# Two stages per slot for the layer tails while the third layer's table is being completed, and one everywhere else

## The chip, the core and the metric

The kernel runs on one core of a Trainium2 chip. The metric is the device time of one execution in microseconds. Inside the core five engines run side by side[...]: TensorE (PE, matrix products), VectorE (DVE), ScalarE (ACT), GpSimd (POOL, which here issues the indirect DMAs and a few small powers) and SyncE (SP, which issues plain DMAs). They wait for each other through semaphores.

## What is computed

Four graph layers follow each other over 8 batches of 2048 nodes with 128 features. The adjacency matrix is sparse: each of its 2048 x 2048 entries is one with probability 1/128, so a node has about 16 neighbours. Layers 0 and 1 are attention layers with 8 heads, a feed-forward part and two layer norms; layers 2 and 3 are graph attention layers with one layer norm.

```python
# layers 0 and 1
scores = jnp.einsum('bnhd,bmhd->bhnm', Q, K) / jnp.sqrt(HEAD_DIM)
scores = jnp.where(mask, -jnp.inf, scores)
attn_out = jnp.einsum('bhnm,bmhd->bnhd', softmax(scores), V)
x = layer_norm(h + (attn_out @ Wo + bo), ln1_g, ln1_b)
x = layer_norm(x + relu(x @ W1 + b1) @ W2 + b2, ln2_g, ln2_b)
# layers 2 and 3
h = x @ W
e = leaky_relu((h @ a_src)[:, :, None] + (h @ a_dst)[:, None, :])
att = softmax(where(adj == 0, -inf, e))
x = ln_gamma * norm(att @ h + x) + ln_beta
```

## The kernel before

The kernel never forms the dense score matrix. At the start it finds the neighbours of every node and sorts the nodes by their number of neighbours. A **tile** t (0 to 15) is 128 nodes of that order, all 8 batches with them; `CAPS` says how many neighbour slots a tile has, 30 for tile 0 down to 11 for tile 15. Each layer l has a **table** in device memory with one row per node (`tables[l]`): keys and values for layers 0 and 1 (2048 numbers), projected features and scores for layers 2 and 3 (1040 numbers). A tile gathers the rows of its neighbours, slot by slot, with an indirect DMA on POOL (`gather`, L320), and works on them.

**Chunks.** The list `every` holds all the work of the four layers in order, cut into chunks: up to 2 neighbour slots in layers 0 and 1, up to 4 in layers 2 and 3. A chunk lies in one of six buffers kv0 to kv5, used in turn. A chunk of layers 2 and 3 (`gat_chunk`) has the stages: small weights and one large product on DVE (L745 to L757), eight scalings by ACT (L762, two batches of each slot), one sum on DVE (L766), and eight matrix products with the identity on PE that add into PSUM (L772).

**Tails.** When a tile's chunks are done, DVE scales the sum (L643 in layers 0 and 1, L649 in layers 2 and 3) and a tail turns it into rows of the next layer's table. A tail is a Python generator, and each `yield` ends one stage. In layers 0 and 1 (`attention_tail`) two halves of a tile (four batches each) run as two tails, the second three stages behind: transposes on PE (L329), a copy on ACT (L666), the residual sum on PE (L674, L678), squares on ACT (L471), a power on POOL (L476, written `rs`), scaling on ACT (L480), transposes, copy (L686), feed-forward (L691, L696, L702 to L712), the second norm (again L471, L476, L480), transposes, copy (L720), projection (L521 to L536) and copies into `rows` (L541 to L547, ACT). In layer 2 (`gat_tail`) one tail does both halves: sums on PE (L793 to L802), squares (L809), one power for both (L836), scaling (L817), transposes, copies (L824) and the same projection. `state_done` then stores the state and loads a later tile's through SP, and `put_rows` writes the rows into the table with an indirect DMA on POOL (L494, called a scatter below) and counts it in `put[l + 1]`. `rows` has one buffer.

**Order.** The order of all instructions is written out by hand. `layers` goes through the chunks; for each it runs stages of the chunk and its neighbours and calls `slot` three times. `slot` (L1103) advances every thread and every tail by one stage and calls `fetch`, which issues the gathers of chunks some four ahead. In the kernel before, every third slot advances the tails once more if `hurry` (L1098) says so: in the last tile of layer 2, and in layers 2 and 3 as long as the table that the layer reads is not complete.

**The start of a layer.** `fetch` does not issue a gather before enough of the table is written. Because most of the table is there when a layer begins, `ORDER` and `EARLY` put first those slots of tiles 0 and 1 whose neighbours lie in the tiles already written. The first eight chunks of layers 2 and 3 are called C1 to C8 here:

- C1, C2, C3, C4: eight slots each of tile 0 and tile 1; they need 13 tiles in the table.
- C5: four slots of tile 0; it needs tile 13 too (14 tiles).
- C6, C7: four slots of tile 0 and of tile 1; they need tile 14 too (15 tiles).
- C8: the folded slots of tile 0 (two gathers); it needs tile 15, so the whole table, as does all that follows.

A scatter into a table waits until all gathers from that table issued before it have landed, and a gather waits until the last scatter before it has landed; `order` below always means the order in an engine's queue. C1 lies in kv2 in layer 2 and in kv5 in layer 3, and the next chunks take the next buffers.

Of the kernel before, what the change touches and what calls it, by code (L numbers as in the profile page):

```python
# [19 lines left out]
NT = N // P  # L20
# [62 lines left out]
def sparse_path(ctx: ExitStack, tc: tile.TileContext, ins: dict, out: bass.AP, flag: bass.AP):  # L83
# [978 lines left out]
    put = [NT, 0, 0, 0]  # L1062
    every = []
    blocks = [[{} for _ in range(NT)] for _ in range(4)]
    for l in range(4):
        per = 2 if l < 2 else 4
        for t, k, ns, folded in pieces(l, per):
            c = dict(l=l, t=t, k=k, ns=ns, folded=folded, box=blocks[l][t])
# [1 line left out]
            c["run"] = (attention_chunk if l < 2 else gat_chunk)(l, c)  # L1070
            every.append(c)
    now = [0, 0]
    beat = [0]

    def advance(group):
        for g in list(group):
            if next(g, 0) == 0:
                group.remove(g)

    def fetch():  # L1080

        while now[1] < len(every):
            c = every[now[1]]
            l, t, k, ns = c["l"], c["t"], c["k"], c["ns"]

            if now[1] - now[0] > (4 if now[1] >= KVB and every[now[1] - KVB]["l"] > 1 else 3):
                return
            resorted = l > 0 and t < 2 and not c["folded"]
            need = NT - max([b for end, b in EARLY[t] if k + ns <= end] + [0] if resorted else [0])
            if put[l] < need:  # L1090
                return
            c["buf"] = buffer()[:, : ns * width(l)].rearrange("p (s c) -> p s c", s=ns)
            for i in range(ns):
                at = t * BASE if resorted else first[t]
                index = (sorted_lists if resorted else lists)[:, at + k + i : at + k + i + 1]
                gather(l, index, c["buf"][:, i])
            now[1] += 1

    def hurry():

        c = every[min(now[0], len(every) - 1)]
        return c["l"] == 2 and c["t"] == NT - 1 or c["l"] > 1 and put[c["l"]] < NT

    def slot():
        advance(threads)
        advance(tails)
        fetch()
        beat[0] += 1
        if beat[0] % 3 == 0 and hurry():
            advance(tails)  # L1110

    def drain():
# [40 lines left out]
    def layers():  # L1153
# [7 lines left out]
        for i in range(len(every) + 2):  # L1161
# [3 lines left out]
            if c["k"] == 0:  # L1165
                l, t = c["l"], c["t"]
                if l == 0:
                    if t + 2 < NT:
                        threads.append(find_lists(t + 2))
                    if t == 0:  # L1170
                        state(0, 1)
                        threads.append(later(12, lambda: state(0, 2) or iter(())))
                        threads.append(later(12, clear_late))
                    if t in (2, 6):
                        threads.append(order_lists(t // 4))
                while l < 2 and "asked" not in c["box"]:
                    slot()
            while i < len(every) and now[1] <= i:
                slot()
# [11 lines left out]
            if c1["l"] in (2, 3) and c1["last"]:  # L1191
                sums(c1["l"], c1["t"], c1["box"])
            go(c)
            slot()
            go(c)
            slot()
# [533 lines left out]
```

## Time and profile before

| | us |
|---|---|
| three runs | 3429.68, 3435.46, 3435.26 (median 3435.26) |
| profiled execution | 3404.58 |
| its span, first to last instruction | 3402.8 |
| mean granted TensorE clock | 0.918 |

Busy time of the engines in three stretches of the profiled execution:

| stretch | from, to (us) | DVE | PE | ACT | POOL | DMA share |
|---|---|---|---|---|---|---|
| inside layer 1 | 1900 to 2000 | 99.32 | 91.78 | 40.09 | 65.41 | 0.79 |
| first product of C1 to first product of C8, layer 2 | 2230.79 to 2327.27 | 44.44 | 65.80 | 45.24 | 40.14 | 0.53 |
| about the same in layer 3 (2788.99 to 2870.17) | 2789 to 2870 | 41.91 | 57.17 | 34.75 | 37.61 | 0.60 |

The numbers under an engine's name are its busy microseconds in the stretch; the share of DMA is the mean of the core's 16 DMA engines. An indirect DMA on POOL is shown with the time in which POOL issues it; its data land later.

### The profile page before, as it was taken

To read this page: it belongs to the slowest core of one execution; us is meant where nothing else is said; L and a number is where in the kernel's file an instruction comes from. 1 tells how busy PE (TensorE), PEld (TensorE's weight loads), DVE (VectorE), ACT (ScalarE), POOL (GpSimd) and SP (SyncE) were. 2 spreads that over 40 slices of the span, in tenths; PEclk is the share of its full clock that TensorE was granted. 3 is DMA by queue.
4 is the path that set the end of the run, shared out by engine and by line. 5 is a ranking of instruction groups with operands and counts; after the bars stand their busy time and mean duration, and the time that the engine had idled before them with its cause. 6 is when DMAs were issued, how large, how long until landed. Compare 5 with 4: busy or idle time off the path is not lost.

```text
span 3402.8 us, 34669 instructions
## 1 busy us (share of the span) xinstructions
PE 2743.1 (81%) x10618; PEld 1582.9 (47%) x10618; DVE 3058.3 (90%) x2695; ACT 1426.6 (42%) x4972; POOL 2207.9 (65%) x1453
## 2 busy tenths in 40 slices
PE   5647888878989997788888989986888976667675
PEld 4523445545555553455545555653445543233332
DVE  7789999999999999999999999976788866889885
ACT  5711333334444442233333444543555654444444
POOL 0065788588657655455676666646787865788773
PEclk9878999999999998899999999998899988888887
DMA  8587787888888777688887888767999986899883
GB/s 336 188 333 266 292 292 282 314 298 288 308 315 299 290 262 295 226 328 295 303 321 295 295 309 299 265 206 250 321 352 346 347 327 223 292 314 330 300 284 112
DMA packets 200625, 986.52 MB, mean 290 GB/s; under 512 B 31918, under 2 KB 33712, under 8 KB 128436
## 3 DMA queue, kind: packets, MB, share of 16 engines
q0 software_dynamic: 175024, 890.45, 72.4%
q1 hardware_dynamic: 20502, 75.52, 5.9%
q10 hardware_dynamic: 4904, 18.24, 1.4%
q8 instruction: 87, 1.43, 0.2%
q14 instruction: 108, 0.88, 0.1%
HBM read 937.16 MB, written 91.55 MB: 302 GB/s over the span
## 4 chain that ended last, share of the span: by engine, by line
DVE 32%; PE 25%; issue 18%; DMA 10%; POOL 5%; ACT 3%; POOLq 0%; DVEq 0%; ACTq 0%
DVE kv L620 11%; DVE kv L606 11%; PE acc L630 8%; PE acc L772 6%; DMA kv<-table,lists 4%; POOL kv L320 3%; DMA kv<-table,sorted_lists 3%; DVE sc L609 2%; PE m L712 2%; DVE kv L766 2%; DMA table<-rows,perm 2%; DVE kv L757 2%; PE m L329 2%; DVE sums L455 1%; DMA out_dram<-rows,perm 1%
## 5 line engine op out<-in xcount | busy, mean ns | idle before, releaser
L320 POOL DMA_INDIRECT kv<-table,lists x955 | 1450.0, 1518 | 357.2 <-issue 206.7
L630 PE MATMUL acc<-kv,ident 128*128 128x512 f32 x2200 | 1107.7, 634 | 222.1 <-DVE kv L620 221.9
L772 PE MATMUL acc<-kv,ident 128*128 128x512 f32 x1184 | 610.1, 667 | 188.6 <-DVE kv L766 155.4
L630 PEld LDWEIGHTS acc<-kv,ident 128*128 128x128 f32 x2200 | 413.7, 202 | 655.1 <-issue 367.5
L606 DVE TENSOR_TENSOR kv<-kv,q 128x2048 f32<-128x2048 f32 (+1 forms) x282 | 629.2, 2231 | 18.7 <-DMA kv<-table,lists 9.7
L609 DVE TENSOR_REDUCE sc<-kv 128x128 f32<-128x2048 f32 (+1 forms) x284 | 634.0, 2232 | 9.2
L620 DVE TENSOR_TENSOR kv<-kv,w 128x2048 f32<-128x2048 f32 (+1 forms) x284 | 631.4, 2223 | 4.9 <-ACT w L615 4.8
L772 PEld LDWEIGHTS acc<-kv,ident 128*128 128x128 f32 x1184 | 243.6, 215 | 504.7 <-issue 285.1
L757 DVE TENSOR_TENSOR kv<-kv,pair 128x3072 f32<-128x3072 f32 (+1 forms) x150 | 466.1, 3108 | 1.0
L476 POOL TENSOR_TENSOR rs<-ss,half 128x4 f32<-128x4 f32 x128 | 221.2, 1728 | 325.4 <-ACT n L471 324.6
L766 DVE TENSOR_TENSOR kv<-kv 128x2048 f32<-128x2048 f32 (+1 forms) x150 | 296.0, 1974 | 129.0 <-ACT kv L762 129.0
L762 ACT ACTIVATE kv<-kv,ws 128x128 f32<-128x128 f32 x1108 | 339.0, 406 | 163.7 <-DVE ws L751 105.5
L471 ACT ACTIVATE n<-m,eps 128x128 f32<-128x128 f32 x512 | 181.0, 366 | 427.1 <-PE m L712 217.4
L615 ACT ACTIVATE w<-sc,lmask 128x64 f32<-128x64 f32 x554 | 165.0, 351 | 455.3 <-DVE sc L609 454.7
L320 POOL DMA_INDIRECT kv<-table,sorted_lists x153 | 204.9, 1339 | 113.0 <-PE acc L630 41.3
L480 ACT ACTIVATE n<-m,rs 128x128 f32<-128x128 f32 x512 | 146.0, 370 | 109.4 <-POOL rs L476 109.0
L494 POOL DMA_INDIRECT table<-rows,perm x57 | 100.2, 1758 | 134.6 <-ACT rows L545 33.5
L329 PE MATMUL m<-ident,n 128*128 128x128 f32 x640 | 106.2, 288 | 73.5 <-ACT n L817 57.2
L712 PE MATMUL m<-w_L_w,hT 128*128 128x128 f32 x1024 | 156.2, 275 | 0.0
L329 PEld LDWEIGHTS m<-ident,n 128*128 128x128 f32 x640 | 82.3, 147 | 140.6 <-ACT n L817 69.0
L712 PEld LDWEIGHTS m<-w_L_w,hT 128*128 128x128 f32 x1024 | 134.9, 192 | 0.0
L691 PE MATMUL m<-n1T,w_L_gnn_W 128*128 128x512 f32 x256 | 131.5, 597 | 0.8 <-ACT n1T L686 0.4
(241 smaller groups left out, 3459.5 us busy)
## 6 DMA issues: line engine op xcount, KB each, us to landing
kept<-xT SPq DMA_DIRECT2D x48, 512.0 KB, 7.4
xT<-kept SPq DMA_DIRECT2D x48, 512.0 KB, 6.8
kv<-in_adj_dram SPq DMA_DIRECT2D x16, 1024.0 KB, 6.7
table<-kv ACTq DMA_DIRECT2D x16, 1024.0 KB, 5.0
kv<-table,lists POOLq DMA_INDIRECT x955, 7.1
kv<-in_x_nodes_dram SPq DMA_DIRECT2D x16, 512.0 KB, 5.8
kv<-table,sorted_lists POOLq DMA_INDIRECT x153, 6.3
found<-cand POOLq DMA_DIRECT2D x16, 64.0 KB, 4.0
```

Source lines behind the costliest of these rows:

```text
L320: nc.gpsimd.indirect_dma_start(out=dst, out_offset=None, in_=tables[l][:, :], in_offset=bass.IndirectOffsetOnAxis(ap=index, axis=0), bound ...
L329: nc.tensor.transpose(pt[:, j * P : (j + 1) * P], src[:, j, :], ident)
L476: nc.gpsimd.tensor_tensor(rs, ss, half[:, :4], op=ALU.pow)
L606: nc.vector.tensor_mul(kk, kk, q[:, None].to_broadcast([P, ns, NB, D]))
L609: nc.vector.tensor_reduce(sc[:, :ns].rearrange("p s (b h) -> p (s b) h", h=NH), kk.rearrange("p s b (h j) -> p (s b) h j", h=NH), axis=AX. ...
L620: nc.vector.tensor_mul(vv, vv, w[:, k : k + ns, :].rearrange("p s (b h) -> p (s b) h", h=NH)[:, :, None, :] .to_broadcast([P, ns * NB, HD, ...
L630: nc.tensor.matmul(acc[:, j, :], merge if c["folded"] else ident, kv[:, i, 4 * j : 4 * j + 4, D:], start=k + i == 0, stop=c["last"] and i ...
L712: nc.tensor.matmul(y[:, j, :], hT[:, f, j, :], wt["2"][:, f, :], start=False, stop=f == 1, skip_group_check=True,)
L757: nc.vector.tensor_mul(hv[:, :, :nv, :], hv[:, :, :nv, :], wc[:, :, :nv, None].to_broadcast([P, ns, nv, D]))
L762: nc.scalar.mul(hv[:, i, b, :], hv[:, i, b, :], ws[:, i, b - nv : b - nv + 1])
L766: nc.vector.tensor_add(hv[:, : ns - left], hv[:, : ns - left], hv[:, left:ns])
L772: nc.tensor.matmul(acc[:, j, :], merge if c["folded"] else ident, hv[:, i, 4 * j : 4 * j + 4, :], start=k + i == 0, stop=c["last"] and i = ...
```

## The change

`hurry` and the counter `beat` go. The tails now take a second stage in every slot, and not in every third, while the current chunk is one of layer 2 and layer 2's table is not complete. In the last tile of layer 2 and at the start of layer 3 they take one stage per slot. Counted over the whole program, the second stage is taken 15 times before (7 at the start of layer 2, 3 in its last tile, 5 at the start of layer 3) and 17 times after, all at the start of layer 2. No operation is added or left out: the change only reorders instructions within the queues of PE, ACT, POOL and SP. DVE's order is the same.

```diff
     now = [0, 0]
-    beat = [0]
...
-    def hurry():
-
-        c = every[min(now[0], len(every) - 1)]
-        return c["l"] == 2 and c["t"] == NT - 1 or c["l"] > 1 and put[c["l"]] < NT
-
     def slot():
         advance(threads)
         advance(tails)
         fetch()
-        beat[0] += 1
-        if beat[0] % 3 == 0 and hurry():
+
+        if now[0] < len(every) and every[now[0]]["l"] == 2 and put[2] < NT:
             advance(tails)
```

## The prediction

> **What bounds the kernel now.** I read the page's busy slices first, then the busy time by stretch, then the waits and the chain of waits at the two places where DVE drops.
>
> ```profile
> DVE  7789999999999999999999999976788866889885
> ...
> DMA  8587787888888777688887888767999986899883
> ```
>
> DVE is at 90% or more nearly everywhere in layers 0 and 1. It falls in slices 27 to 29 (2210 to 2470 us) and 33 to 34 (2720 to 2890 us), where layers 2 and 3 begin; DMA falls with it, so neither is the limit there. By stretch (PE, PEld, DVE, ACT, POOL):
>
> ```profile
> 2230.79:2327.27 96.48, 65.80 (x318) 42.41 (x316) 44.44 (x41) 45.24 (x171) 40.14 (x39) 0.86 0.53 176
> 2789.00:2870.00 81.00, 57.17 (x222) 32.43 (x220) 41.91 (x37) 34.75 (x140) 37.61 (x29) 0.87 0.60 211
> ```
>
> No engine is full: both stretches are chains of latency, 52 and 39 us of DVE idle. The waits in the first, then the second stretch:
>
> ```profile
> DVE kv L745 <- DMA kv<-table,lists: 23.7, 1, 23.7
> POOL rs L476 <- ACT n L471: 23.4, 3, 12.0
> ...
> POOL table L494 <- DMA kv<-table,sorted_lists: 7.9, 1, 7.9
> ```
> ```profile
> DVE kv L766 <- ACT kv L762: 40.7, 7, 10.8
> PEld m L329 <- ACT n L817: 30.7, 3, 12.5
> ACT n L817 <- POOL rs L836: 30.7, 3, 13.0
> ...
> POOL table L494 <- ACT score L547: 13.6, 1, 13.6
> ```
>
> In layer 2 DVE waits 23.7 us for C8's gathers, so for the scatter of tile 15. In layer 3 almost all comes from one thing: ACT stands at L817 until POOL has done the power L836, and everything behind it on ACT waits, L762 first. POOL is late because gathers stand ahead of the power and wait for a scatter. POOL's timeline shows it (the last column is its idle time and what ended it):
>
> ```profile
> 2803.94 1.01 POOL L494 DMA_INDIRECT table<-rows,perm  x1 [7.36 <-DMA kv<-table,sorted_lists]
> 2804.97 1.67 POOL L836 TENSOR_TENSOR rs<-ss,half 128x8 f32<-128x8 f32 x1
> ...
> 2820.58 2.33 POOL L494 DMA_INDIRECT table<-rows,perm  x1 [5.96 <-ACT rows L545]
> 2828.54 1.03 POOL L320 DMA_INDIRECT kv<-table,sorted_lists  x1 [5.63 <-DMA table<-rows,perm]
> ...
> 2839.88 1.67 POOL L836 TENSOR_TENSOR rs<-ss,half 128x8 f32<-128x8 f32 x1
> 2855.12 2.36 POOL L494 DMA_INDIRECT table<-rows,perm  x1 [13.56 <-ACT score L547]
> ```
>
> The scatters are those of tiles 13, 14, 15, the powers those of tiles 14 and 15. Tile 15's squares end at 2830.3 (ACT's timeline), its power runs 9.6 us later, behind C6's and C7's eight gathers; from there to its scatter are 15.2 us.
>
> **What the Trainium skill says.** "Perfetto Trace Analysis", section "DMA Instruction — SWDGE (GPSIMD)": the profiler's end of such a DMA is when the last descriptor is generated, not when the data have moved. The trace agrees: scatters of 1.0 to 2.4 us on POOL release their readers 4.3 (at 2267.88) to 7.2 us (at 2820.58) after the start. "TensorE: Matmul & The Clock Gate", section "Architectural detail: the array is 16× 32×32, not 1× 128×128", under "Engine queue depths": ACT, DVE and each GpSimd core are strict FIFO. So a power behind gathers waits for them: L836 starts at 2839.88, 0.02 us after the last of the eight.
>
> **The change part by part.** Only queues are reordered; the built program shows the orders. POOL at the start of layer 3 (g is four gathers, s a scatter, p a power; numbers are tiles):
>
> ```
> before: s12 gC1 p13 gC2 gC3 gC4 s13 p14 gC5 s14 gC6 gC7 p15 s15 gC8
> after:  s12 gC1 p13 gC2 gC3 gC4 p14 s13 gC5 p15 s14 gC6 gC7 s15 gC8
> ```
> and at the start of layer 2 (two halves: a, b; the second norm has a prime):
> ```
> before: p14'b gC5 s14 p15a gC6 gC7 p15b p15'a p15'b s15 gC8
> after:  p14'b gC5 s14 gC6 gC7 p15a p15b p15'a p15'b s15 gC8
> ```
>
> *Start of layer 3* (times on the old axis; the two orders are the same up to 2779.92, the first L817 of tile 13). Each tail stage falls behind a later chunk, and the powers 14 and 15 move ahead of a scatter.
> - ACT after its first L817 (1.14 us) does L762 of tile 15's second chunk (2.44) at once: done 2783.4, so DVE's L766 starts 2.2 us earlier than 2785.60. PE then loses its later gaps of 6.1 and 11.6 us (at 2807.10 and 2842.01, both for L817).
> - s13 stays at 2803.9: it waits for C4's gathers, the last issued at 2795.58 and landing 7.56 us later. p14 needs squares at 2796.7 and runs in that wait, free.
> - s13's landing (2808.1) frees the one `rows` buffer. Then on ACT: L541 to L547 0.9, L824 0.6, L762 2.4, L809 1.4, L541 0.5; PE L793 to L802 1.9; ACT L809 1.5; POOL p15 1.7: 2808.3 + 10.9 = 2819.2, so s14 goes at about 2819.5 against 2820.58, 1.1 earlier. C5's gathers have landed (2813.63 + 5.54 = 2819.2). o of tile 15 (L649), at 2814.28 before behind the L329 that waited for L817, now needs only PE's sums of the last chunk, about 2803, so it does not hold p15.
> - From s14 the last of the eight gathers is issued 18.3 us later as before (2820.58 to 2838.87), now 2837.8. The 13.56 us of waiting for tile 15's rows go; what is late next is the landing of C7's gathers, 8.1 us as the chain shows for four gathers (2258.97 to 2267.08): 2845.9. The rows are ready before: L762 of C6 stands ahead of the last L541 on ACT and waits for C6's gathers (last issued 2832.6, landed 2840.7), then 0.9 + 2.4 + 0.9 = 2844.9. Margin 1.0.
> - s15 2845.9 against 2855.12: 9.2 us. C8 follows 14.85 us after s15 (2855.12 to DVE at 2869.97), and DVE has C7 done by 2853. I take **-9.2**. Bounds: the landing of s14 has been 4.3 to 9.3 us (2763.18) where I use the 7.2 of the old s14: -2.9, +2.1; p15 late by 3 us through PE running its matmuls at the slow rate after a pause (L772 x8 took 6.10 at 2808.14 against 3.60): +3. So -12 to -4.
>
> *Last tile of layer 2*: the three stages given up move only copies and squares around L762; POOL's order there is the same and s12 waits for a DMA. Nothing, with the wait of p13 behind s12 as cover; without it 2 us (one slot, a third of a 6.2 us chunk: 0.55 small products, 3.35, 2.29).
>
> *Start of layer 2*: the table is complete five slots earlier in the code; what counts is the queues.
> - p14'b: with both L696 ahead of C1's L762 (2.44), ACT is at L480 and L471 at 2252.0 instead of 2252.6. gC5 and s14 are 0.6 earlier: s14 2267.3.
> - Tile 15's first power now stands behind the eight gathers: 2283.9, not 2268.92. The second, at 2284.43 before, comes after ACT's first L480 and second L471 (1.1 + 1.4): about 2287.5. ACT stands still meanwhile, C4's L762 behind it, until 2289.7 (2271.0 before).
> - From the first power: scaling 1.1, squares 1.4, L686 0.6, power 1.05, scaling 1.1, L762 2.4, two L696 and L686 1.9: 2293.7. Then PE: C3's L772 to 2294.8, L702 to L712 3.0, two L691 1.8, L696 0.6, L702 to L712 3.0: 2303.2; ACT C5's L762 and L471 to 2305.5; power 1.05, scaling 1.15: 2307.8; PE's projection is through L527 at 2308.2; ACT L541 to L547 1.4, L720 0.6, C6's L762 2.4, L541 to L545 0.9: rows at about 2313.6. s15 2313.9 against 2314.22.
> - So the stages gained are given back by the powers' place on POOL: **-0.3**. Bounds: each ACT-PE handover may hold 0.3 us more, some ten of them, and PE may run slow for one L772 more: +5; PE at full rate from the start: -4. The delayed L762 push C3 to C7 on DVE, done by 2315, and DVE waits for C8 to 2326: that cover is 11 us.
>
> *SP*: each moved stage 20 takes a state's store and load with it, 0.32 us of issue each, tiles ahead of use; nothing. The rest of layers 2 and 3 keeps its order and shifts as a whole.
>
> Sum: -9.2 - 0.3 = -9.5 on the profiled execution of 3404.58: 3395.1. That execution is 0.9% below the median of the runs, so in the same ratio 3435.26 x 3395.1 / 3404.58 = **3425.7**.
>
> **Rivals.**
> - *Both starts gain.* Layer 2's table really comes five slots earlier: 5 x 2.07 = 10.3, with layer 3's 9.2: 3415.6. For it: PE and ACT idle between stages there. Against: POOL's order and the landing of gC5, which I see unmoved.
> - *It nets out.* s14 of layer 3 lands late or its readers meet a busy queue (gain 5), and layer 2 loses 2: -3, 3432. For it: landings spread over 5 us in this one trace. Against: C7's landing allows 9.
> - *Slower: p15 holds s14.* In layer 3 POOL now cannot issue s14 before tile 15's squares. If those came one chunk later than before (2830.3 + 6.2), as the code's slots have it, p15 ends 2838.2, s14 goes at 2838.3, s15 18.3 + 8.1 later at 2864.7, 9.6 later than now: 3445. It costs from squares later than 2826.9 and decides from 2834. For it: the removed stages. Against: most of the 2830.3 was waiting for L817, which the new order takes away.
> - That the change does nothing: excluded by the orders above.
>
> **How the numbers follow.** Forecast 0.63 (own range 3420 to 3431), both gain 0.09, nets out 0.18, slower 0.10. Range: 3417 to 3434, leaving out the slower case and tails of the two others. About 0.2%, 6.9 us, is what can be told from no change. Faster by more: 0.56 of the forecast, 0.09, 0.03 of the third: 0.68. Slower by more: 0.11. Within: 0.21.
>
> **What would show it.** Right: in layer 3 s15 some 9 us nearer to p13 (76.9 us before, about 68), waiting for gathers and not for ACT; p15 ahead of s14; the L817 waits on L836 fall from 30.7 to under 16 us. In layer 2 both first powers directly behind eight gathers, and s15 within 4 us of 46.3 after s14. Wrong: s14 of layer 3 waiting for p15 with C5 long landed, or C8 of layer 2 moving by more than 5 us.

## The result, and the profile after

Over 14 runs of each, taken side by side, the changed kernel takes 3423.38 us (3415.98 to 3429.37) and the kernel before 3433.75 us (3426.85 to 3441.48): a ratio of 0.9969, 95% interval 0.996 to 0.9978, so 7.5 to 13.7 us faster, 10.6 in the middle. The forecast was 3425.7 us, 9.5 us faster on its own scale.

The two profiled executions can't be set against each other as wholes: the one of before had a span of 3402.8 us, the one of after has 3415.0, although the kernel is faster. Where those 12 us come from is shown at the end; it is not at the two places that the change touches. So the reading goes stretch by stretch, each from an event inside the stretch.

The page of the changed kernel, busy tenths in 40 slices:

```profile
DVE  8789999999999999999999999957777975889885
...
DMA  8587778888888777687887887757998997899883
```

The two dips are still there: slices 27 to 31 and 33 to 34. The change didn't make either start of a layer busy; it made the second one shorter. Busy time by stretch of the changed kernel (PE, PEld, DVE, ACT, POOL, granted clock, DMA share, GB/s), C1's first product to C8's in layer 2, and the same pair of events in layer 3:

```profile
2230.84:2328.99 98.15, 66.87 (x318) 42.67 (x316) 44.36 (x41) 45.60 (x171) 41.92 (x40) 0.85 0.52 180
2808.56:2884.50 75.94, 55.58 (x240) 34.32 (x238) 41.96 (x38) 36.47 (x146) 33.98 (x32) 0.88 0.66 236
```

The first line is the one of before over again: 98.15 us against 96.48 with the same work. In layer 3 the same work of DVE (41.91 us before, 41.96 now) lies in 75.9 us where it lay in 81.0. The waits say why, layer 2's start first (us in total, times, longest), in the kernel before:

```profile
ACT n L480 <- POOL rs L476: 19.6, 3, 10.2
...
DVE kv L766 <- ACT kv L762: 14.1, 6, 5.1
```

and in the changed kernel:

```profile
DVE kv L766 <- ACT kv L762: 36.5, 6, 18.7
ACT n L480 <- POOL rs L476: 27.7, 5, 15.7
...
DVE kv L745 <- DMA kv<-table,lists: 11.9, 1, 11.9
```

and layer 3's start from p13 to C8, in the changed kernel:

```profile
POOL rs L836 <- ACT n L809: 17.1, 2, 9.5
...
ACT n L817 <- POOL rs L836: 11.6, 1, 11.6
...
DVE kv L745 <- DMA kv<-table,lists: 7.7, 1, 7.7
```

In layer 3, counted from p13 (the power of tile 13) on, ACT's wait for the power falls from 30.7 us in three waits to 11.6 in one, and that one is tile 13's, which was there before (13.0). The direction has turned: POOL now waits for the squares of ACT (17.1), not ACT for POOL. In layer 2 a wait has moved instead: DVE waited 23.7 us for C8 before and waits 11.9 now, but ahead of that it has now stood 18.7 us at L766 of C4 (5.1 was its longest wait at L766 before), because ACT stands 15.7 us at L480 for a power. POOL's timeline of the changed kernel, layer 2, has the reason (the last column is idle time and what ended it):

```profile
2269.81 1.76 POOL L494 DMA_INDIRECT table<-rows,perm  x1 [8.19 <-ACT n L471]
2274.69 1.03 POOL L320 DMA_INDIRECT kv<-table,sorted_lists  x1 [3.12 <-DMA table<-rows,perm]
...
2283.81 0.99 POOL L320 DMA_INDIRECT kv<-table,sorted_lists  x1 [0.30 <-issue]
2284.83 1.04 POOL L476 TENSOR_TENSOR rs<-ss,half 128x4 f32<-128x4 f32 x1
...
2315.12 2.37 POOL L494 DMA_INDIRECT table<-rows,perm  x1 [6.10 <-ACT score L547]
```

Tile 15's first power runs 0.03 us after the last of the eight gathers ends; its squares were done at 2269.75. That the profile names these squares (L471) as what ended the 8.19 us ahead of the scatter s14 is a coincidence in time: in the profile of layer 2's part they end 0.6 us before s14 starts, and in the second profile of the kernel with two powers ahead (both below) they end after it; s14 goes 9.2 us after the last gather of C5, where it went 8.9 us after it before. And POOL in layer 3 of the changed kernel:

```profile
2826.51 1.66 POOL L836 TENSOR_TENSOR rs<-ss,half 128x8 f32<-128x8 f32 x1 [7.58 <-ACT n L809]
2828.37 1.06 POOL L494 DMA_INDIRECT table<-rows,perm  x1 [0.20 <-issue]
...
2847.26 1.68 POOL L836 TENSOR_TENSOR rs<-ss,half 128x8 f32<-128x8 f32 x1 [9.50 <-ACT n L809]
2849.14 1.06 POOL L494 DMA_INDIRECT table<-rows,perm  x1 [0.20 <-issue]
2853.34 1.02 POOL L320 DMA_INDIRECT kv<-table,sorted_lists  x1 [3.15 <-PE m L329]
...
2871.12 1.02 POOL L494 DMA_INDIRECT table<-rows,perm  x1 [7.67 <-DMA kv<-table,sorted_lists]
```

The last line is what the prediction asked for: s15 waits 7.67 us for C7's gathers, where it waited 13.56 us for ACT. The two scatters s13 and s14, though, stand directly behind p14 and p15, and these wait for squares: the mechanism of the slower rival is there, at a small price. Whether that price is real is asked by one of the experiments.

### The profile page after: what moved, and what is told of

It is laid out like the page before. It is cut to its first block, busy times and chain, and to the rows that moved or that the text cites. A ratio compares the mean times of both kernels' runs of the same rounds, so it can differ in the third digit from the quotient of the medians.

```text
span 3415.0 us, 34673 instructions
## 1 busy us (share of the span) xinstructions
PE 2759.5 (81%) x10618; PEld 1591.8 (47%) x10618; DVE 3058.4 (90%) x2695; ACT 1428.9 (42%) x4972; POOL 2206.5 (65%) x1453
## 4 chain that ended last, share of the span: by engine, by line
DVE 38%; PE 23%; issue 19%; DMA 11%; POOL 4%; ACT 4%; POOLq 0%; ACTq 0%; DVEq 0%; another core or an unknown queue 0%; SPq 0%
DVE kv L620 13%; DVE kv L606 13%; PE acc L772 7%; PE acc L630 5%; DMA kv<-table,lists 4%; POOL kv L320 3%; DVE sc L609 3%; DMA kv<-table,sorted_lists 2%; DVE kv L766 2%; DMA out_dram<-rows,perm 2%; DVE kv L757 2%; PE m L329 2%; DVE sums L455 2%; PE m L712 1%; PE m L512 1%
## 5 line engine op out<-in xcount | busy, mean ns | idle before, releaser
L757 DVE TENSOR_TENSOR kv<-kv,pair 128x3072 f32<-128x3072 f32 (+1 forms) x150 | 466.2, 3108 | 1.0
L476 POOL TENSOR_TENSOR rs<-ss,half 128x4 f32<-128x4 f32 x128 | 232.7, 1818 | 319.0 <-ACT n L471 318.2
L766 DVE TENSOR_TENSOR kv<-kv 128x2048 f32<-128x2048 f32 (+1 forms) x150 | 296.2, 1975 | 138.4 <-ACT kv L762 131.1
L471 ACT ACTIVATE n<-m,eps 128x128 f32<-128x128 f32 x512 | 181.4, 367 | 428.0 <-PE m L712 215.7
L480 ACT ACTIVATE n<-m,rs 128x128 f32<-128x128 f32 x512 | 146.4, 370 | 131.1 <-POOL rs L476 130.6
L494 POOL DMA_INDIRECT table<-rows,perm x57 | 95.5, 1676 | 112.8 <-ACT rows L518 26.3
```

The costliest lines, as they stand in the source:

```text
L476: nc.gpsimd.tensor_tensor(rs, ss, half[:, :4], op=ALU.pow)
L757: nc.vector.tensor_mul(hv[:, :, :nv, :], hv[:, :, :nv, :], wc[:, :, :nv, None].to_broadcast([P, ns, nv, D]))
L766: nc.vector.tensor_add(hv[:, : ns - left], hv[:, : ns - left], hv[:, left:ns])
```

## The experiments

Theory A is the prediction's: layer 3's start gives the whole gain, layer 2's start nothing, since there both first powers of tile 15 stand behind eight gathers. Its rivals: both starts gain; layer 2 loses and layer 3 gives more; and, for what is left, D: p14 and p15 hold the scatters.

Each row has one profile. The table gives, from POOL's and DVE's timelines, the distances between the starts of the instructions named in the prediction (C1 is its first product L757, C8 its first product's small one L745; us).

| kernel | ratio to before (95%) | L2: s14 to s15 | L2: C1 to C8 | L3: p13 to s13 | s13 to s14 | s14 to s15 | s15 to C8 | p13 to C8 |
|---|---|---|---|---|---|---|---|---|
| before | 1 | 46.3 | 96.0 | 25.7 | 16.6 | 34.5 | 14.6 | 91.5 |
| changed | 0.9969 (0.996 to 0.9978) | 45.3 | 97.6 | 28.4 | 20.8 | 22.0 | 12.9 | 84.1 |
| layer 3's part | 0.9969 (0.996 to 0.9978) | 46.8 | 97.6 | 27.9 | 18.0 | 23.3 | 12.8 | 82.0 |
| layer 2's part | 0.9998 (0.9988 to 1.0009) | 45.8 | 97.1 | 26.3 | 16.4 | 32.6 | 14.9 | 90.2 |
| powers late in layer 3 | 0.9974 (0.9966 to 0.9983) | 46.3 | 94.6 | 27.8 | 16.9 | 25.9 | 13.0 | 83.6 |
| two powers ahead | 0.9928 (0.9911 to 0.9945) | 31.9 | 81.6 | 28.0 | 17.1 | 23.2 | 13.1 | 81.4 |
| the same once more | 0.9923 (0.9906 to 0.994) | 33.7 | 83.6 | 28.4 | 16.2 | 23.4 | 12.8 | 80.7 |
| one power ahead | 0.996 (0.9946 to 0.9975) | 41.2 | 91.9 | 27.8 | 18.5 | 23.1 | 12.8 | 82.2 |
| two ahead, few stages | 0.995 (0.9937 to 0.9964) | 38.8 | 91.8 | 27.6 | 16.9 | 22.9 | 12.8 | 80.2 |
| three powers ahead | 0.9933 (0.9915 to 0.9951) | 35.6 | 85.5 | 27.6 | 17.0 | 22.9 | 12.6 | 80.2 |
| two ahead, two row buffers | 0.9916 (0.9898 to 0.9933) | 31.5 | 81.9 | 27.9 | 16.2 | 23.1 | 12.9 | 80.2 |
| layer 3's start alone | 0.9978 (0.9964 to 0.9992) | 47.1 | 96.9 | 27.0 | 19.3 | 26.4 | 12.8 | 85.5 |
| one stage everywhere | 0.9977 (0.9967 to 0.9988) | 46.6 | 102.6 | 28.1 | 18.3 | 23.2 | 12.6 | 82.1 |

### Each half of the change alone

Layer 3's part, against the kernel before:

```diff
-        return c["l"] == 2 and c["t"] == NT - 1 or c["l"] > 1 and put[c["l"]] < NT
+        return c["l"] == 2 and put[2] < NT
```

> Only layer 3's part of the change: the start of layer 2 keeps its second stage in every third slot, the last tile of layer 2 and the start of layer 3 take one stage per slot. Theory A (the prediction's: layer 3 gives about all of it, layer 2 about nothing): 8 to 10 us faster than the kernel before, a ratio of 0.9971 to 0.9977, within 2 us of the changed kernel; in the trace C8 of layer 3 is 82 to 85 us behind p13 (91.8 before), and s15 of layer 2 is 46 us behind s14 as before. Rival B (both starts gain): about half, 4 to 6 us, 0.9983 to 0.9988. Rival C (the gain is made up of both, and layer 2 loses as much as its extra stages suggest): more than the whole change, 12 us or better, 0.9965 or less.

Layer 2's part, against the kernel before:

```diff
-        if beat[0] % 3 == 0 and hurry():
+        if now[0] < len(every) and every[now[0]]["l"] == 2 and put[2] < NT or beat[0] % 3 == 0 and hurry():
```

> Only layer 2's part of the change: two stages in every slot at the start of layer 2, and the second stage of every third slot kept in the last tile of layer 2 and at the start of layer 3. Theory A: nothing, -1 to +2 us against the kernel before, a ratio of 0.9997 to 1.0006, and C8 of layer 3 92 us behind p13 as before. Rival B: 4 to 10 us faster, 0.997 to 0.9988. Rival C: 2 to 5 us slower, 1.0006 to 1.0015.

Layer 3's part gives 0.9969, just the changed kernel's ratio, and layer 2's part 0.9998, an interval of 0.9988 to 1.0009 that reaches 4 us to the faster side and 3 to the slower. Rival B wanted 4 to 10 us there and is left with the edge of the interval. C wanted 12 us or more from layer 3 and a loss of 2 to 5 in layer 2; by the time it too is left with the edges of both intervals (0.996 and 1.0009). The distances speak for A: with layer 3's part p13 to C8 falls to 82.0 us, with layer 2's part s14 to s15 (45.8) and C1 to C8 (97.1) stay near 46.3 and 96.0. So theory A holds for where the gain lies, and the times don't contradict it.

### Do the powers hold the scatters in layer 3?

The changed kernel, with the powers of tiles 14 and 15 one stage later; the scalings that read them stay where they are (L839 in this kernel is the L836 of the others):

```diff
         squares(1)
+        late = l == 2 and t >= NT - 2
+        if late:
+            yield
         nc.gpsimd.tensor_tensor(rs, ss, half, op=ALU.pow)
-        for _ in range(3):
+        for _ in range(2 if late else 3):
             yield
```

> The changed kernel with the powers of tiles 14 and 15 in layer 3 issued one stage later, so that POOL has s13 p14 and s14 p15 where the change made p14 s13 and p15 s14; nothing moves on ACT, PE and DVE. Theory D (the scatters s13 and s14 are held by powers whose squares come late): s13 goes when C4's gathers have landed, 2 to 3 us earlier, s14 when C5's have, another 3 to 5 us earlier, and C8 of layer 3 is 76 to 80 us behind p13 (84.1 in the changed kernel); 4 to 8 us faster than the changed kernel, a ratio to the kernel before of 0.9946 to 0.9958. Rival E (landing times and a busy ACT hold s13 and s14 in any case, and L817 now waits longer for the later powers): no better than the changed kernel, 0.9969 or above, C8 84 us or more behind p13.

0.9974 is not better than the changed kernel, so D's 4 to 8 us aren't there. POOL's timeline of this kernel from s13 on:

```profile
2806.04 1.01 POOL L494 DMA_INDIRECT table<-rows,perm  x1 [7.93 <-DMA kv<-table,sorted_lists]
2807.07 1.68 POOL L839 TENSOR_TENSOR rs<-ss,half 128x8 f32<-128x8 f32 x1
...
2822.97 1.00 POOL L494 DMA_INDIRECT table<-rows,perm  x1 [6.25 <-ACT score L547]
2826.49 1.68 POOL L839 TENSOR_TENSOR rs<-ss,half 128x8 f32<-128x8 f32 x1 [2.52 <-ACT n L809]
2828.86 3.07 POOL L320 DMA_INDIRECT kv<-table,sorted_lists  x1 [0.68 <-PE acc L772]
```

s13 goes no earlier (27.8 us behind p13; it waits for C4's gathers), and s14 neither (16.9 us behind s13, within the 16.2 to 18.5 that all profiles of the change's order show but the changed kernel's own). Instead p15 now stands between s14 and C6's gathers: its squares end at 2826.3, and the first gather goes 5.9 us behind s14, not 4.2 as in the changed kernel. So E's "no better" holds (its 84 us or more from p13 to C8 was missed by a little: 83.6); the run doesn't say what the scatters would gain if nothing were put in the gathers' way. The changed kernel's own profile is an outlier: there p14 comes 26.5 us behind p13, in the seven other profiles of its order with one buffer of rows 18.8 to 22.0. Its PE ran L797 and L802 ahead of p14's squares in 1.91 and 1.92 us after a pause of 4.97 us, against 1.02 and 1.05 for the next tile's; but the kernel with two powers ahead and few stages has them slow there too (1.78 and 1.92), with p14 21.9 us behind p13. What sets the outlier apart from it are two waits of ACT just before: 1.67 us at L809 and 2.75 us at L541, the second for something that the trace doesn't name (none and 1.09 us at the same places of the other kernel). Why they came is open.

### Only the start of layer 3, and no second stage at all

In the first, only the second stages at layer 3's start are given up (those of layer 2's last tile stay); in the second, `hurry` and its `advance` are left out, so that layer 2's start too has one stage per slot.

```diff
-        return c["l"] == 2 and c["t"] == NT - 1 or c["l"] > 1 and put[c["l"]] < NT
+        return c["l"] == 2 and (c["t"] == NT - 1 or put[2] < NT)
```

> Only the second stages at the start of layer 3 are given up; those of the last tile of layer 2, and layer 2's start, are as in the kernel before. POOL has s13 p14 and s14 p15 in layer 3. Theory A (the last tile of layer 2 is worth nothing): as the run of layer 3's part, a ratio to the kernel before of 0.9963 to 0.9977. Rival L (the stages given up in the last tile are what brings p14 and p15 ahead of the scatters, and that is the gain): half the gain or less, 0.998 or above.

> One stage per slot everywhere, at the start of layer 2 too; layer 3 as in the changed kernel. It tells what the second stages at layer 2's start are worth in the order before. Theory A: tile 14's scatter falls behind two more powers and comes one or two chunks later, 5 to 12 us lost against layer 3's part alone: a ratio to the kernel before of 0.9983 to 1.0004. Rival M (the start of layer 2 runs at the gathers' pace and the stages there do not matter): as layer 3's part alone, 0.9963 to 0.9977.

0.9978 (0.9964 to 0.9992) lies on the border of A and L: against the changed kernel's 0.9969 the last tile is worth 3 us by the medians, anything from nothing to some 8 by the intervals, and 3 to 5 us by p13 to C8 (85.5, where the three kernels of the change's order on the same chip have 80.2, 82.1 and 82.2). It does decide the order: with the last tile's stages kept, POOL has s13 p14 and s14 p15, the order of the kernel with late powers, which has 83.6. In both, p15 stands behind s14 but ahead of the eight gathers, and most of the way from 91.5 to 81.6 is there. So "nothing" for the last tile was too little, and L's "half the gain" isn't excluded by the interval. One stage everywhere, 0.9977 (0.9967 to 0.9988), doesn't tell its two theories apart by the time either (A 0.9983 and above, M 0.9977 and below; the median is M's). Its profile has C1 to C8 of layer 2 at 102.6 us, 5 to 8 us longer than all with the old or the changed order: by the profile the second stages there are worth something, at the lower end of what A said; by the time that isn't resolved.

### Taking the powers out from behind the gathers

If layer 2's extra stages are lost because two powers stand behind eight gathers, then holding back the gathers, not the powers, must bring the time out. The gathers that need tile 14 are issued only once tile 15's powers are counted (`powers` grows by one after each L476 of its tail; only the deciding line is shown, and the added one moves the lines below L476 down by one, so that L494 is L495 here):

```diff
-            if put[l] < need:
+            if put[l] < need or l == 2 and need == NT - 1 and blocks[1][NT - 1].get("powers", 0) < 2:
                 return
```

> The changed kernel with the eight gathers of C6 and C7 in layer 2 held back until the first powers of both halves of tile 15 are issued, so POOL has s14 p15a p15b gC6 gC7 in place of s14 gC6 gC7 p15a p15b. Theory A (the extra stages gain nothing because both powers stand behind the eight gathers): L480 of tile 15 goes at about 2273 instead of 2285.9 on the trace's axis, the gathers go 1 to 3 us later, s15 is 33 to 40 us behind s14 instead of 45.3, and C8 of layer 2 some 5 to 9 us earlier: a ratio to the kernel before of 0.9943 to 0.9955. Rival F (layer 2 is held by the gathers' own pace or by DVE and ACT with C3 to C7, the powers' place is no matter): s15 less than 3 us nearer to s14, time as the changed kernel's within 2 us, 0.9963 to 0.9975. Rival G (later gathers cost more than they bring): slower than the changed kernel, 0.9975 or above.

> The kernel that held back C6's and C7's gathers in layer 2 behind both first powers, run once more beside the two variants of it. Theory A: a ratio to the kernel before of 0.991 to 0.9945 again, s15 31 to 34 us behind s14 in layer 2, C8 of layer 3 80 to 84 us behind p13. If its earlier gain lay in a lucky set of runs: above 0.9955.

0.9928 and, on another chip, 0.9923: 24 to 26 us faster than before, and by the ratios 14 to 16 us better than the changed kernel's 0.9969. It beats both kernels, and by more than A expected: C8 of layer 2 came 14 to 16 us earlier, not 5 to 9. No operation was added. POOL's timeline of the kernel with two powers ahead:

```profile
2265.32 1.66 POOL L495 DMA_INDIRECT table<-rows,perm  x1 [8.14 <-ACT n L471]
2267.01 1.05 POOL L476 TENSOR_TENSOR rs<-ss,half 128x4 f32<-128x4 f32 x1
2270.87 1.01 POOL L476 TENSOR_TENSOR rs<-ss,half 128x4 f32<-128x4 f32 x1 [2.82 <-ACT n L471]
2272.05 1.07 POOL L320 DMA_INDIRECT kv<-table,sorted_lists  x1 [0.18 <-issue]
...
2282.74 0.99 POOL L320 DMA_INDIRECT kv<-table,sorted_lists  x1 [0.30 <-issue]
2283.76 1.04 POOL L476 TENSOR_TENSOR rs<-ss,half 128x4 f32<-128x4 f32 x1
...
2297.21 2.38 POOL L495 DMA_INDIRECT table<-rows,perm  x1 [5.73 <-ACT score L548]
```

The gathers could not have gone before s14 had landed anyway: in the changed kernel the first stands 4.9 us behind s14's start. Both powers fit into that gap but for 1.9 us (first gather 6.7 us behind s14). On ACT the scaling follows at once; the changed kernel's line first,

```profile
2285.91 1.14 ACT L480 ACTIVATE n<-m,rs 128x128 f32<-128x128 f32 x4 [15.69 <-POOL rs L476]
```

then the same line in the kernel with two powers ahead:

```profile
2268.09 1.14 ACT L481 ACTIVATE n<-m,rs 128x128 f32<-128x128 f32 x4 [2.45 <-POOL rs L476]
```

The 15.69 us of standing fall to 2.45, and s15 comes 12 to 13 us nearer to s14. F and G are out. That each GpSimd core takes its queue strictly first in, first out is what the Trainium skill says ("TensorE: Matmul & The Clock Gate", section "Architectural detail: the array is 16× 32×32, not 1× 128×128", under "Engine queue depths"). The changed kernel's trace agrees: there a power of 1.04 us waited 15.1 us (2269.75 to 2284.83) for gathers that themselves waited for a landing.

Which of the two powers counts? The same with `"powers" not in` the tile in place of `< 2`, so that one power is enough:

> The changed kernel with the eight gathers of C6 and C7 in layer 2 held back only until the first power of tile 15's first half is issued: POOL has s14 p15a gC6 gC7 p15b. It tells whether the first power alone frees the chain, or both are needed. Theory H (each power counts by when it runs; the second still stands behind the eight gathers): p15b runs at once behind the last gather, some 1 to 3 us earlier than in the changed kernel, s15 41 to 44 us behind s14 (45.3 in the changed kernel, 31.9 with both powers ahead), a ratio to the kernel before of 0.9958 to 0.9968. Rival I (what counts is that ACT does not stand at the first L480 for 15.7 us, with the chunk's L762 behind it): s15 32 to 37 us behind s14 and a ratio of 0.9928 to 0.9945.

0.996, s15 41.2 us behind s14: H, not I. ACT was freed of its long stand at the first power, and still s15 came only 4.1 us nearer and by the medians only 3 us were won on the changed kernel (the intervals overlap), because the second half's power now stood directly behind the gathers (ACT's longest wait for a power was 10.2 us, for that one). The later of two halves sets the end.

And what are the second stages worth once the powers are out of the way? The `< 2` condition, with layer 2's second stage in every third slot as before:

> Both first powers of tile 15 ahead of C6's and C7's gathers in layer 2, as in the run that held them back, but the second stage at layer 2's start taken only in every third slot as in the kernel before; layer 3 as in the changed kernel. It tells what the extra stages are worth once the powers are out of the gathers' way. Theory J (the stages matter as soon as the powers do not hold them): the gathers go 2 to 4 us later than with two stages per slot, s15 35 to 41 us behind s14, a ratio to the kernel before of 0.9938 to 0.9955. Rival K (the extra stages are worth nothing even then; the order on POOL is all): s15 31 to 33 us behind s14 and a ratio of 0.9922 to 0.9935.

0.995, 38.8 us: J. The powers' place alone brings about 7.5 us from s14 to s15 (46.3 or 46.8 to 38.8), the extra stages then another 5 to 7 (to 31.9 and 33.7); in the ratios the second step is 0.995 to 0.9928 and 0.9923, with intervals that just overlap. So the stages of layer 2 are worth something, and in the change POOL's order took it back.

Does it pay to hold the gathers back further? Three powers ahead (`< 3`):

> As the kernel that held back C6's and C7's gathers in layer 2 until two powers of tile 15 are issued, but until three are (p15'a too). It looks for the limit of the cover. Theory P (the gathers may be late only until s15's rows wait for nothing but them: they would start some 10 us later, end about 29 us after s14 and land 8 us later, and the fourth power stands behind them): s15 37 to 42 us behind s14 (31.9 with two powers ahead), 4 to 9 us slower than with two, still faster than the changed kernel. Rival Q (DVE and ACT have enough slack, gathers 10 us later cost nothing): s15 30 to 33 us behind s14, same time within 3 us.

0.9933 beside 0.9923 of the same set, intervals overlapping; s15 35.6 us behind s14, between what P and Q said and nearer to P. P's reason was half right: s15 still waits for ACT's rows (7.37 us), not for the late gathers. The fourth power now stands directly behind them, at 2297.45; that this makes s15 late is likely, but no run moved it.

### The buffer of rows

On top of two powers ahead, the rows of layer 2's tiles take two buffers in the space that held the queries of layers 0 and 1 (widened by 16 numbers; the lines of that are left out here):

```diff
-            box["rows"] = work.tile([P, NB * 2 * D], F32, tag="rows", name="rows", bufs=1)
+            two = box["l"] == 2
+            shape = [P, NB * D + 2 * NB] if two else [P, NB * 2 * D]
+            box["rows"] = work.tile(shape, F32, tag="q" if two else "rows", name="rows", bufs=2 if two else 1)
```

> The kernel that held back C6's and C7's gathers behind both first powers in layer 2, with a second buffer for the rows of layer 2's tiles, so that a tile's copies L541 to L547 no longer wait until the scatter of the tile before has been read out. It asks what still separates the scatters at layer 3's start. Theory N (after s13 the chain is landing of s13, four gathers, their landing: rows are ready by then or nearly so): s14 15 to 17 us behind s13 (17.1 before the second buffer), C8 79 to 82 us behind p13 (81.4), time within 3 us of the kernel with one buffer. Rival O (the one buffer of rows makes the chain from s13 to s14): s14 11 to 14 us behind s13, C8 75 to 78 us behind p13, 4 to 7 us faster than the kernel with one buffer.

0.9916 beside 0.9923, the same within the intervals, and s14 16.2 us behind s13 as with one buffer in that set: N. In this kernel's POOL timeline

```profile
2795.65 1.06 POOL L495 DMA_INDIRECT table<-rows,perm  x1 [7.19 <-DMA kv<-table,sorted_lists]
2800.87 1.02 POOL L320 DMA_INDIRECT kv<-table,sorted_lists  x1 [4.16 <-DMA table<-rows,perm]
...
2811.88 1.06 POOL L495 DMA_INDIRECT table<-rows,perm  x1 [3.29 <-DMA kv<-table,sorted_lists]
2816.09 2.00 POOL L320 DMA_INDIRECT kv<-table,sorted_lists  x1 [3.15 <-DMA table<-rows,perm]
...
2835.01 1.02 POOL L495 DMA_INDIRECT table<-rows,perm  x1 [7.84 <-DMA kv<-table,sorted_lists]
2839.51 1.61 POOL L320 DMA_INDIRECT kv<-table,lists  x1 [3.48 <-DMA table<-rows,perm]
```

every scatter waits for gathers and every first gather for a scatter: from s13 on, layer 3's start is now landings and the issue of gathers between them, and the tails no longer show in it.

## Why the prediction was right

- **Layer 3, -9.2: the size holds, four of its parts don't.** Eight profiles with the change's order and one row buffer have p13 to C8 at 80.2 to 84.1, mean 81.6; the two with the old order 91.5 and 90.2, mean 90.8: -9.2. Four of the eight come from chips that run the stretch before p13 as fast as the two old ones do (last section); these alone give 81.1, so -9.8. The parts, in means of all eight, are p13 to s13 +2.0 (predicted 0, "s13 stays at 2803.9"), s13 to s14 +1.3 (predicted -1.1), s14 to s15 -10.6 (predicted -8.1), s15 to C8 -1.9 (predicted 0).
  - The first: from the start of C4's last gather to s13 it takes 9.2 to 10.6 us in the seven new profiles in which s13 waits for gathers, where it took 8.4 and 8.9 in the two old ones; why is open.
  - The second: s14 was to go 15.6 us behind s13 and goes 16.2 to 18.5, 20.8 once; in five of the eight it follows p15's end within 0.7 us, in three it still waits 2.2 to 2.5 us after p15 for C5's gathers, so both of its conditions come later than in the sum (p15 starts 13.2 to 18.9 us behind s13, 13.6 in the list of steps).
  - The third and fourth: the landings. Behind s14 the sum used the 7.2 of the old s14, with 4.3 as the lower bound; in the changed kernel the first gather goes 4.2 us behind s14, and 4.2 behind s15 as well (5.5 before).
  - These are errors of +4.4 and -4.4 us that cancel: the size was right in part by luck. The sign, and the limit on s15 (C7's gathers in place of ACT), were not luck. That p15's place ahead of the eight gathers is what gives it is read from the orders and the waits; no run moved p15 alone back behind them.
- **Layer 2's start, -0.3: holds from s14 on, step by step.** s14 to the first power was to be 16.6 us and was 15.0, to the second 20.2 and 18.8, to s15 46.6 and 45.3; over the three profiles with this order 45.3 to 46.3, where the old order has 46.3 to 47.1. C1 to C8 is 96.4 in the mean of these three, 96.8 in the three with the old order: -0.4, within a spread of 3 us. The 0.6 us by which s14 itself was to come earlier don't show (37.4 us behind C1's first product in the mean of the three, 37.3 before). One line of the working doesn't add up: from the first power at 2283.9 its terms give 2293.5, or 2294.5 with the power's own 1.05 us, where it has 2293.7; that is inside its bounds. The cover was put at 11 us; DVE still waits 11.9 us for C8.
- **Last tile of layer 2, 0:** this term was too small. The place of p14 and p15 ahead of the scatters, which the sum credits to the start of layer 3, depends on these stages. With them kept, p13 to C8 is 85.5, some 5 us less than in the old order; the -9.2 belongs to both places together, and perhaps 3 to 5 us of it to the last tile, which isn't resolved in time.
- **The rivals.** Both starts gain: not seen as the change stands (layer 2's part alone 0.9998), though the 10 us that it hoped for in layer 2 exist behind the gathers. Nets out: its mechanism (s14 lands late) went the other way. p15 holds s14: seen in the profile, at up to 4 us between s13 and s14, far from the 9.6 that it needed; moving p15 back behind s14 brought nothing that shows.
- **The signs.** s15 came 5.7 us nearer to p13 in the changed kernel's own profile (71.2), 7 to 10 in the others with its order and one buffer (67.4 to 69.5), against the predicted 9. L817's waits fell to 11.6. (The 30.7 before is from p13 on; in the stretch that the prediction names, from 2789 on, it is 17.6 in two waits.) The sign of "wrong", s14 waiting for p15, did appear, and wasn't decisive. C8 of layer 2 moved by 1.7 us on the trace's axis, inside the 5 allowed.

## What to carry to other kernels

When a schedule hands out more stages and nothing comes of it, look at what stands behind a blocked instruction on the queue that all of them share: here two powers of 1 us each behind eight gathers cost some 14 us, and holding back the gathers, which were blocked for 5 us anyway, brought more than the whole change. Free the last of the parallel halves, not only the first, or most of the gain is lost: here one power ahead brought s15 4.1 us nearer, two 12 to 13. And cost a chain that alternates scatters and gathers by its landings, with their spread, before counting stages.

## What the runs showed of the hardware

The same program takes different times on different chips, and at a particular place. On three chips the kernel before had medians of 3405.29, 3406.38 and 3429.81 us. The stretch of layer 2 from C8 to p13 of layer 3, whose order the change leaves alone but for its last tile, took 449 to 453 us in all seven profiles of the first two chips, whichever kernel it was, and 468 to 475 in all four of the third. The profile of before, with 451.4, is of the first kind, that of after, with 471.5, of the second: these 20 us, of which the start of layer 3 gives 7.4 back, are where their 12 us of difference in span come from, the other way round to the kernels' times. Its busy time in the kernel before, then in the changed one (PE, PEld, DVE, ACT, POOL, granted clock, DMA share, GB/s):

```profile
2328.00:2778.00 450.00, 379.01 (x1408) 209.81 (x1408) 387.74 (x412) 247.79 (x968) 355.79 (x273) 0.93 0.94 339
```

```profile
2329.80:2799.90 470.10, 393.36 (x1408) 219.48 (x1408) 387.60 (x412) 248.79 (x967) 349.52 (x272) 0.91 0.92 324
```

DVE and ACT do the same work in the same time; PE needs 14 us more at a lower granted clock, and DMA moves the same data at 324 instead of 339 GB/s. Which of the two causes the other wasn't tried. Its practical use: compare two profiles only stretch by stretch, and times only within runs of one chip; the ratios held across chips (0.9928 and 0.9923).
